# Column tiles for five matmul steps of a conv, spectral attention and FFN kernel, with a new table of times

## The chip, the cores and the metric

The kernel runs on one core of a Trainium2 chip. The metric is the device time of one execution in microseconds (us). The time before is the median of three runs; the profile is of one more execution.

## The reference

The input x is 64 images of 96 channels, 56 x 56 pixels. Two layers follow each other.

```python
# layer 0: a convolution block (MID = 192)
out = silu(bn(einsum('bchw,oc->bohw', x, expand_w)))
out = channel_shuffle(shift_groups(out), groups=4)
dw  = bn(depthwise 3x3 of out)
out = silu(bn(dw + bn(out * id_w)))
out = out * sigmoid(grouped_1x1(relu(grouped_1x1(mean(out)))))
x   = silu(bn(einsum('bchw,oc->bohw', out, proj_w)) + x)
# layer 1: on tokens t of (64, 3136, 96)
t = t + attn(layernorm(t))
t = t + ffn(layernorm(t))
```

The attention is a spectral filter: a linear map w1 to 192 hidden values with ReLU, a Fourier transform over the 3136 tokens, a complex map with a ReLU per frequency (diagonals of r and i, biases rb and ib), the inverse transform, and a linear map w2 back to 96 channels, with batch norms folded in. The FFN has 384 hidden values; the inputs and weights of its products are rounded to an 8-bit float.

## The kernel before

One image is cut into 56 kinds of steps, most of them repeated for several groups of the image. `STEPS` lists the functions, and `PLAN` gives for each call of each step a due time, relative to the image. The time of image b is moved by `b * PERIOD`. The program is written in the order of these times, and every engine carries out its own part of that order:

```python
        for _, b, k, i in sorted(
            (b * PERIOD + when, b, k, i)
            for b in range(NB)
            for k, step in enumerate(STEPS)
            for i, when in enumerate(PLAN[step.__name__])
        ):
            STEPS[k](b, i)
```

So the steps of three to four images lie among each other, and the table alone decides what stands ahead of what on an engine. Semaphores between the engines follow from the tiles that a step reads and writes.

The names of steps end in their kind: `_mm` are matmuls, `_ev` evictions of PSUM by ScalarE or VectorE. The steps that matter here, in the order of one image:

- `c_mm` and `n_mm`, by `centred` (L546): the centring products of the two layer norms. 112 tokens at a time are the stationary operand, the table `center` of 96 columns streams. Four such matmuls fill one bank of the pool `psb`; `squared` (L551, ScalarE) and `variance` (L555, VectorE) follow.
- `w1_mm` (L613): 64 columns of t are loaded for each of two halves of w1; the halves go to PSUM partitions 0 to 63 and 64 to 127.
- `f1_mm` (L640): the transform along rows, 64 columns of `buf_h` loaded of which 56 are a row, twice (real and imaginary part), 58 columns streaming.
- `f2_mm` (L666 for the first 128 hidden values, L670 for the last 64): the second transform, with `l_tab` of 112 columns streaming.
- `w2_mm` (L724 for the first 128 hidden values, L736 for the last 64, in two row halves): the map back, 112 columns of the stationary operand, 96 streaming.
- `i1_mm` (L765) and `i2_mm` (L787): the inverse transform in two steps. `i2_mm` loads 64 columns of which 48 are channels, in two tiles of 64 rows by 64 columns.

The other steps that take TensorE time are the expand products `ea_mm` (L373) and `eb_mm` (L390), the depthwise taps `dw_mm` (L436), the projection `pj_mm` (L522, L527), and the FFN: `x_mm` (L831), `h_mm` (L844), `o_mm` (L866).

PSUM is split in two. The pool `psa` has two buffers of 1024 float32 values per partition, [...] for `w1_mm`, `f1_mm`, `f2_mm`, `w2_mm`, `i1_mm` and `i2_mm`. The pool `psb` has four buffers of one bank, for all others.

## Time and profile before

| | |
|---|---|
| median of 3 runs | 7661.35 us (7661.08 to 7678.29) |
| span of the profiled execution | 7642.9 us |
| granted TensorE clock | 0.992 |
| TensorE (PE) busy | 7490.6 us |
| weight loads (PEld) busy | 5769.2 us |
| VectorE (DVE) busy | 5011.6 us |
| ScalarE (ACT) busy | 4675.8 us |
| GpSimd (POOL) busy | 1530.9 us |
| HBM read, written | 82.80 MB, 77.07 MB |

Busy time is the time in which an engine had at least one instruction at work. The matmuls overlap each other, so the busy time of a group of matmuls is not what the group costs: that is read from the distances between the starts of pieces in the timeline. A piece is a run of instructions of the same line. The chain of waits is followed back from the last instruction, and says which engine held up the end.

### The profile page before, as it was taken

The numbers are of one execution on the slowest core, as the hardware profiler recorded it, in microseconds if no ns is written. First come the engines' busy times: TensorE is split into PE (matmuls) and PEld (weight loads), VectorE is DVE, ScalarE is ACT, GpSimd is POOL, SyncE is SP. The second block draws the span as 40 slices with busy tenths as digits, with TensorE's granted clock in tenths as the row PEclk, the third lists the DMA queues.
The fourth block names the chain that finished last, engine by engine and source line by source line (L and its number), as shares of the span: only waits on it lengthen the run. The fifth ranks groups of instructions, "written<-read, shape, count | busy, mean of one in ns | idle before, by whom it ended". The sixth has DMA issues, their size and how long they took to land.

```text
span 7642.9 us, 347263 instructions
## 1 busy us (share of the span) xinstructions
PE 7490.6 (98%) x159362; PEld 5769.2 (75%) x159362; DVE 5011.6 (66%) x8793; ACT 4675.8 (61%) x9806; POOL 1530.9 (20%) x1360
## 2 busy tenths in 40 slices
PE   7999999999999999999999999999999999999997
PEld 4777777777777777777777777777777777777776
DVE  5666666666666666666666666666666666666665
ACT  3565565665665656656656566566565665665656
POOL 0111212212112122122121221221212212212112
PEclk9999999999999999999999999999999999999998
DMA  1110101101101101011011010110110101101100
GB/s 45 22 24 21 25 21 24 26 19 27 24 21 26 25 21 26 19 27 25 20 27 24 21 25 19 27 25 20 27 24 21 25 21 25 27 18 27 24 21 20
DMA packets 424192, 183.03 MB, mean 24 GB/s; under 512 B 378785, under 2 KB 422041, under 8 KB 422473
## 3 DMA queue, kind: packets, MB, share of 16 engines
q1 hardware_dynamic: 420970, 155.82, 8.9%
q8 instruction: 1251, 20.50, 1.1%
q10 hardware_dynamic: 1264, 3.48, 0.1%
q14 instruction: 211, 1.73, 0.1%
q0 software_dynamic: 496, 1.50, 0.1%
HBM read 82.80 MB, written 77.07 MB: 21 GB/s over the span
## 4 chain that ended last, share of the span: by engine, by line
PE 94%; ACT 3%; issue 1%; DVE 1%; DMA 0%; POOL 0%; POOLq 0%; SPq 0%; ACTq 0%; DVEq 0%
PE ps_d L436 13%; PE ps_f L640 10%; PE ps_w L613 8%; PE ps_i L787 6%; PE ps_eb L390 5%; PE ps_w L724 5%; PE ps_n L546 5%; PE ps_ea L373 5%; PE ps_c L546 5%; PE ps_pj L522 5%; PE ps_i L765 5%; PE ps_f L666 5%; PE ps_h L844 3%; PE ps_w L736 3%; PE ps_o L866 3%; PE ps_f L670 3%
## 5 line engine op out<-in xcount | busy, mean ns | idle before, releaser
L882 POOL TENSOR_TENSOR o<-t,o 112x448 f32<-112x448 f32 x448 | 632.7, 1418 | 4108.2 <-DVE o L876 2577.0
L555 DVE TENSOR_REDUCE v<-sq 112x4 f32<-112x384 f32 x896 | 492.7, 550 | 891.7 <-ACT sq L551 883.6
L436 PE MATMUL ps_d<-e_a,diag 32*32 32x392 f32 x36864 | 1034.3, 498 | 1.4 <-ACT d L446 0.7
L854 DVE TENSOR_SCALAR y<-y,qb 128x448 f16<-128x448 f16 x1344 | 594.3, 457 | 583.6 <-ACT y L849 575.6
L458 DVE SCALAR_TENSOR_TENSOR d_last<-e_b,taps,d_last 128x1568 f32<-128x1568 f32 x512 | 947.2, 1850 | 13.7
L436 PEld LDWEIGHTS ps_d<-e_a,diag 32*32 32x32 f32 x36864 | 661.1, 103 | 301.1 <-issue 45.1
L849 ACT CAST y<-ps_h 128x448 f16<-128x448 f32 x1344 | 715.1, 544 | 139.3 <-PE ps_h L844 137.0
L640 PE MATMUL ps_f<-f_tab,buf_h 128*64 128x58 f32 x24576 | 770.9, 223 | 0.2 <-DVE buf_h L625 0.2
L640 PEld LDWEIGHTS ps_f<-f_tab,buf_h 128*64 128x64 f32 x24576 | 737.2, 138 | 34.3 <-issue 25.8
L860 ACT CAST h<-y 128x448 fp8e5<-128x448 f16 x1344 | 739.7, 579 | 10.6 <-DVE y L854 10.2
L816 POOL TENSOR_TENSOR rs<-v,mhalf 112x4 f32<-112x4 f32 x448 | 448.9, 1007 | 1343.6 <-DVE v L556 1343.6
L613 PE MATMUL ps_w<-w1c,t 112*64 112x96 f32 x14336 | 650.8, 248 | 0.4 <-DVE buf_h L625 0.4
L613 PEld LDWEIGHTS ps_w<-w1c,t 112*64 112x64 f32 x14336 | 602.2, 137 | 18.6 <-issue 1.4
L573 POOL TENSOR_TENSOR rs<-v,mhalf 112x4 f32<-112x4 f32 x448 | 446.7, 1011 | 624.5 <-DVE v L556 624.0
L652 ACT COPY buf_g<-ps_f 128x464 f32<-128x464 f32 x768 | 395.7, 551 | 271.5 <-PE ps_f L640 263.3
L625 DVE SCALAR_TENSOR_TENSOR buf_h<-ps_w,rs_full 128x768 f32<-128x768 f32 (+1 forms) x512 | 431.4, 853 | 133.3 <-PE ps_w L613 133.2
L533 DVE TENSOR_TENSOR ps_pj<-ps_pj,x 112x392 f32<-112x392 f32 x512 | 261.4, 567 | 380.0 <-PE ps_pj L527 363.2
L551 ACT ACTIVATE sq<-ps_n 112x384 f32<-112x384 f32 x448 | 219.7, 490 | 453.5 <-PE ps_n L546 452.9
L666 PEld LDWEIGHTS ps_f<-l_tab,buf_g 128*128 128x128 f32 x3712 | 443.9, 192 | 68.7 <-ACT h L860 34.5
L546 PEld LDWEIGHTS ps_c<-center,t 112*112 112x112 f32 x3584 | 398.4, 180 | 109.1 <-ACT buf_h L776 79.8
L539 ACT ACTIVATE t<-ps_pj,pjbn_b 112x392 f32<-112x392 f32 x512 | 288.1, 618 | 308.2 <-DVE ps_pj L533 308.1
L666 PE MATMUL ps_f<-l_tab,buf_g 128*128 128x112 f32 x3712 | 462.3, 277 | 3.9 <-DVE ue L704 3.3
(174 smaller groups left out, 13514.1 us busy)
## 6 DMA issues: line engine op xcount, KB each, us to landing
x<-in_x SPq DMA_DIRECT2D x896, 84.0 KB, 2.8
out_dram<-o SPq DMA_DIRECT2D x896, 84.0 KB, 2.0
l_tab<-in_tab_l ACTq DMA_DIRECT2D x1, 1624.0 KB
r_tab<-in_tab_r ACTq DMA_DIRECT2D x1, 1568.0 KB
t<-dev_t SPq DMA_DIRECT2D x64, 7.0 KB, 1.8
t<-dev_t SPq DMA_DIRECT2D x64, 5.2 KB
ex_row_p<-in_expand_row POOLq DMA_DIRECT2D x1, 336.0 KB, 4.3
s_p<-in_bn POOLq DMA_DIRECT2D x1, 288.0 KB, 3.8
```

Of the source, the lines that this page charges most:

```text
L436: nc.tensor.matmul(pss[r][j * 32 : j * 32 + 32], lhsT=diag[pr, tap, :], rhs=e_a[pr, r0 : r0 + PJ, dx : dx + HW], start=tap == 0, stop=tap ...
L458: nc.vector.scalar_tensor_tensor(d_last, win, w, d_last, ALU.mult, ALU.add)
L546: nc.tensor.matmul(cen[:, k, 0:C], lhsT=t_of(b)[:, n0 : n0 + CP], rhs=center, start=True, stop=True)
L555: nc.vector.tensor_reduce(v, sq, AX.X, ALU.add)
L613: nc.tensor.matmul(ps[hc * 64 : hc * 64 + 64, k, 0:C], lhsT=t[:, n0 : n0 + 64], rhs=w1c[:, hc * C : hc * C + C], start=True, stop=True,)
L640: nc.tensor.matmul(ps[r * 64 : r * 64 + 64, k, 0 : 2 * NK], lhsT=buf_h[:, n0 : n0 + 64], rhs=f_tab[:, r, :], start=True, stop=True,)
L666: nc.tensor.matmul(ps[:, k, 0:CP], lhsT=g_v[:, k1, 0:128], rhs=l_tab[:, k1, :], start=True, stop=True)
L787: nc.tensor.matmul(ps[pr, bk, k, 0:HW], lhsT=buf_h[pr, n2 * 48 : n2 * 48 + 64], rhs=r_tab[pr, n2, :], start=True, stop=True,)
L849: nc.scalar.copy(y16, held.pop(("h", b, i)))
L854: nc.vector.tensor_scalar(y16, y16, qb1[:, i % 3 : i % 3 + 1], 0.0, ALU.add, ALU.max)
L860: nc.scalar.copy(held["h8", b, j][:, m, :], held.pop(("y", b, i)), saturate=False)
L882: nc.gpsimd.tensor_tensor(o32, rows, o16, ALU.add)
```

## The change

Four edits go together.

1. `c_mm`, `n_mm`, both products of `w2_mm`, and `f2_mm` for the first 128 hidden values run in two column tiles. The stationary operand is cut at column 64, and the two parts write PSUM partitions 0 to 63 and 64 up. The products are the same, the number of matmuls is doubled.
2. `f1_mm` loads the 56 columns of a row and no longer 64, and `i2_mm` loads 48 and no longer 64. The partitions in between are then not written any more, though the evictions still read them.
3. So that these partitions hold finite values from the start, the two buffers of `psa` are now fixed tiles, set to zero once, and `mix_ps` gives them out in turn.
4. `PERIOD` and `PLAN` are new: 122.718 becomes 116.056, and nearly every due time moves, so that the steps are written in another order.

The diff without the table:

```diff
+TILES = ((0, 64), (64, CP))
...
-PERIOD = 122.718
+PERIOD = 116.056
...
-    psa = ctx.enter_context(tc.tile_pool(name="psa", bufs=2, space=PSUM))
+    psa = ctx.enter_context(tc.tile_pool(name="psa", bufs=1, space=PSUM))
...
+    psa_buf = [psa.tile([128, 1024], F32, tag=f"psa_{i}", name=f"psa_{i}") for i in range(2)]
+    for ps in psa_buf:
+        nc.vector.memset(ps, 0.0)
+
+    def mix_ps(**shape):
+        psa_buf.reverse()
+        return psa_buf[0].rearrange(f"p ({' '.join(shape)}) -> p {' '.join(shape)}", **shape)
...
-            nc.tensor.matmul(cen[:, k, 0:C], lhsT=t_of(b)[:, n0 : n0 + CP], rhs=center, start=True, stop=True)
+            for c0, c1 in TILES:
+                nc.tensor.matmul(
+                    cen[c0:c1, k, 0:C], lhsT=t_of(b)[:, n0 + c0 : n0 + c1], rhs=center, start=True, stop=True
+                )
...
-        ps = psa.tile([128, 8, 128], F32, tag="psa", name="ps_w1")
+        ps = mix_ps(b=8, c=128)
...
-        ps = psa.tile([128, 16, 64], F32, tag="psa", name="ps_f1")
+        ps = mix_ps(c=16, k=64)
...
-                    ps[r * 64 : r * 64 + 64, k, 0 : 2 * NK],
-                    lhsT=buf_h[:, n0 : n0 + 64],
+                    ps[r * 64 : r * 64 + HW, k, 0 : 2 * NK],
+                    lhsT=buf_h[:, n0 : n0 + HW],
...
-                nc.tensor.matmul(ps[:, k, 0:CP], lhsT=g_v[:, k1, 0:128], rhs=l_tab[:, k1, :], start=True, stop=True)
+                for c0 in (0, 64):
+                    nc.tensor.matmul(
+                        ps[c0 : c0 + 64, k, 0:CP],
+                        lhsT=g_v[:, k1, c0 : c0 + 64],
+                        rhs=l_tab[:, k1, :],
+                        start=True,
+                        stop=True,
+                    )
...
-                nc.tensor.matmul(
-                    ps[:, u, k, 0:C],
-                    lhsT=pq_a[:, AT[k1], :],
+                for c0, c1 in TILES:
+                    nc.tensor.matmul(
+                        ps[c0:c1, u, k, 0:C],
+                        lhsT=pq_a[:, AT[k1], c0:c1],
...
-                if k < len(rows):
+                for c0, c1 in TILES if k < len(rows) else ():
                     pr = slice(u * 64, u * 64 + 64)
                     nc.tensor.matmul(
-                        ps[:, u, k, 0:C],
-                        lhsT=pq_b[pr, low[k], :],
+                        ps[c0:c1, u, k, 0:C],
+                        lhsT=pq_b[pr, low[k], c0:c1],
...
-                        ps[pr, bk, k, 0:HW],
-                        lhsT=buf_h[pr, n2 * 48 : n2 * 48 + 64],
+                        ps[oh * 64 : oh * 64 + 48, bk, k, 0:HW],
+                        lhsT=buf_h[pr, n2 * 48 : n2 * 48 + 48],
```

More of the change, by code (lines that the diff above doesn't have):

```diff
@@ L37 @@
 AT = {k: i for i, k in enumerate(ROWS)}
-PERIOD = 122.718
+PERIOD = 116.056
 PLAN = {
-    "x_in": (-147.721, -151.744, -149.471, -138.934, -151.822, -125.323, -138.247),
-    "ea_mm": (-141.029, -145.082, -126.726, -119.750, -120.807, -120.941, -120.290),
-    "ea_ev": (-138.555, -140.044, -126.163, -116.583, -120.200, -120.739, -114.561),
-    "eb_mm": (-121.730, -112.705, -108.018, -102.565, -105.002),
-    "eb_ev": (-120.973, -111.659, -106.503, -100.444, -101.911),
-    "dw_mm": (-79.917, -78.566, -78.565, -65.087, -63.669, -63.339),
-    "dw_ev": (-73.802, -73.487, -71.759, -70.033, -59.506, -57.515, -59.275, -57.457),
-    "lt": (-98.023, -96.293, -96.292, -92.859, -92.644, -88.886, -84.859, -75.675, -75.445),
-    "ls": (-61.863,),
-    "se1_mm": (-52.796,),
-    "se1_ev": (-50.943,),
-    "se2_mm": (-49.672,),
-    "se2_ev": (-48.379,),
-    "se2_th": (-46.770,),
-    "se2_pw": (-43.096,),
-    "pj_mm": (-41.772, -41.568, -32.605, -31.242),
-    "pj_add": (-40.396, -41.539, -38.890, -38.801, -31.213, -30.588, -31.045, -29.469),
-    "pj_ev": (-39.434, -38.301, -37.756, -35.301, -30.149, -29.022, -29.487, -27.900),
-    "c_mm": (-24.146, -21.968, -25.583, -16.009, -16.007, -11.503, -13.696),
-    "c_sq": (-22.682, -14.839, -23.121, -14.926, -13.660, -10.792, -11.392),
-    "c_v": (-20.883, -14.495, -18.980, -14.647, -13.137, -10.398, -11.322),
-    "c_pow": (-18.019, -14.194, -13.743, -13.702, -8.813, -8.176, -5.296),
-    "sp_v": (-10.789, -3.853),
-    "sp_mm": (-6.118, -0.681),
-    "sp_ev": (-4.506, -0.256),
-    "w1_mm": (-0.346, -0.212, 4.672, 7.510, 5.475, 12.909, 19.419, 18.928),
-    "w1_ev": (1.860, 1.106, 6.745, 17.019, 7.900, 13.580, 21.053, 22.482),
-    "f1_mm": (23.538, 26.705, 26.665, 29.311, 30.272, 32.515),
-    "f1_ev": (26.424, 25.244, 29.624, 29.156, 28.725, 26.695, 29.658, 29.859, 35.164, 35.095, 35.471, 35.913),
-    "f2_mm": (38.580, 41.391, 46.368, 52.795, 60.421, 66.169),
-    "f2_u": (40.203, 42.708, 44.419, 46.131, 57.356, 57.983, 57.453, 58.671, 64.502, 65.061, 72.435, 73.918),
-    "f2_s": (40.310, 43.807, 44.675, 46.796, 58.705, 58.706, 60.334, 60.335, 71.712, 71.894, 72.991, 75.274),
-    "f2_r": (46.995, 48.118, 58.706, 62.406, 79.686, 75.565),
-    "f2_p": (51.508, 57.047, 61.277, 69.180, 80.050, 85.487),
-    "w2_mm": (77.959, 76.224, 83.328, 86.566),
-    "w2_ev": (82.557, 79.792, 87.523, 92.017),
-    "i1_mm": (93.204, 96.670, 99.124),
-    "i1_ev": (96.030, 106.024, 102.973),
-    "i2_mm": (107.109, 107.592, 117.276, 118.471),
-    "i2_ev": (109.058, 110.782, 109.796, 112.025, 118.147, 119.865, 120.548, 122.140),
-    "n_mm": (112.633, 113.049, 118.802, 125.828, 130.991, 134.196, 139.651),
-    "n_sq": (112.809, 113.222, 120.133, 125.855, 132.488, 134.747, 139.729),
-    "n_v": (113.661, 114.505, 120.979, 128.480, 132.611, 135.903, 140.002),
-    "n_pow": (114.812, 115.024, 122.305, 128.819, 133.543, 139.096, 140.278),
-    "n_x": (117.079, 117.343, 122.642, 131.969, 137.995, 139.881, 144.238),
-    "x_mm": (118.765, 123.606, 126.764, 139.293, 142.364, 146.447, 144.732),
-    "x_ev": (122.340, 123.815, 132.084, 139.673, 148.954, 151.364, 145.152),
@@ new lines @@
+    "x_in": (-142.751, -132.334, -138.890, -139.641, -151.208, -133.652, -137.370),
+    "ea_mm": (-127.116, -124.446, -119.920, -94.498, -104.745, -112.167, -106.964),
+    "ea_ev": (-125.252, -124.279, -119.721, -94.105, -94.974, -110.456, -105.960),
+    "eb_mm": (-110.852, -109.364, -102.468, -94.672, -100.705),
+    "eb_ev": (-109.889, -108.508, -98.175, -94.671, -100.704),
+    "dw_mm": (-77.186, -75.415, -71.686, -59.708, -58.836, -58.630),
+    "dw_ev": (-67.184, -68.088, -65.354, -62.005, -53.949, -53.481, -53.376, -53.432),
@@ new lines @@
+    "lt": (-93.236, -91.843, -90.397, -86.333, -83.176, -78.618, -75.060, -71.072, -58.358),
+    "ls": (-56.957,),
+    "se1_mm": (-52.674,),
+    "se1_ev": (-52.590,),
+    "se2_mm": (-49.560,),
+    "se2_ev": (-47.764,),
+    "se2_th": (-46.882,),
+    "se2_pw": (-44.842,),
+    "pj_mm": (-44.604, -44.263, -36.259, -33.499),
+    "pj_add": (-41.623, -41.337, -40.573, -40.255, -32.468, -30.814, -32.509, -32.127),
+    "pj_ev": (-41.036, -40.637, -40.429, -36.736, -30.334, -29.230, -31.146, -29.797),
@@ new lines @@
+    "c_mm": (-24.403, -20.404, -19.123, -17.297, -18.726, -9.644, -8.872),
+    "c_sq": (-23.198, -19.663, -17.391, -16.366, -11.963, -8.651, -8.871),
+    "c_v": (-21.831, -17.939, -17.390, -11.021, -10.842, -8.366, -8.657),
+    "c_pow": (-19.058, -12.292, -10.931, -8.952, -1.526, -3.948, -1.526),
+    "sp_v": (-8.951, -1.525),
+    "sp_mm": (-6.057, 0.802),
+    "sp_ev": (-5.461, 1.113),
+    "w1_mm": (1.423, -2.619, 3.588, 18.203, 8.943, 12.171, 13.999, 16.535),
+    "w1_ev": (3.273, -0.045, 7.600, 20.920, 11.591, 14.999, 15.957, 19.212),
@@ new lines @@
+    "f1_mm": (21.608, 26.248, 24.638, 31.810, 32.559, 32.004),
+    "f1_ev": (25.169, 25.895, 30.841, 28.844, 27.556, 26.595, 32.009, 32.411, 36.910, 36.732, 36.699, 35.929),
+    "f2_mm": (37.220, 36.994, 44.528, 54.196, 60.721, 63.959),
+    "f2_u": (39.991, 41.910, 38.664, 38.665, 56.185, 56.316, 56.071, 58.643, 62.858, 62.962, 66.464, 67.055),
+    "f2_s": (42.369, 43.646, 41.684, 42.524, 58.496, 59.412, 59.011, 59.603, 66.349, 66.780, 67.365, 69.133),
+    "f2_r": (44.699, 46.227, 59.499, 60.966, 71.228, 72.985),
@@ new lines @@
+    "f2_p": (46.153, 47.154, 60.124, 60.967, 72.402, 74.345),
+    "w2_mm": (70.359, 71.061, 73.352, 79.154),
+    "w2_ev": (70.421, 73.788, 79.483, 82.773),
+    "i1_mm": (82.811, 83.639, 91.924),
+    "i1_ev": (86.931, 93.317, 99.344),
+    "i2_mm": (102.107, 101.737, 110.644, 111.766),
+    "i2_ev": (106.004, 107.037, 104.651, 104.395, 113.248, 110.645, 115.503, 113.393),
+    "n_mm": (109.042, 108.523, 116.336, 120.505, 126.604, 126.539, 137.374),
+    "n_sq": (109.105, 109.021, 116.337, 120.506, 127.174, 126.540, 137.375),
@@ L90 @@
+    "n_v": (109.642, 109.022, 116.338, 120.507, 127.975, 126.902, 138.122),
+    "n_pow": (110.809, 110.170, 116.496, 122.658, 132.126, 129.135, 139.318),
+    "n_x": (112.520, 110.693, 119.248, 123.053, 133.298, 130.929, 139.362),
+    "x_mm": (113.125, 114.113, 121.321, 126.216, 135.244, 138.382, 142.002),
+    "x_ev": (114.896, 115.709, 126.025, 126.217, 137.926, 142.365, 142.302),
     "h_mm": (
-        151.663, 153.691, 155.645, 157.017, 158.080, 157.809, 173.388, 173.148, 174.630, 194.728, 189.826, 193.482,
@@ L92 @@
-        196.505, 206.300, 207.755, 217.228, 217.688, 219.518, 219.352, 222.352, 220.276,
+        144.408, 144.539, 142.955, 151.653, 146.123, 151.741, 165.593, 167.081, 167.021, 179.037, 181.701, 184.163,
+        183.315, 191.401, 194.122, 202.572, 203.025, 214.978, 205.482, 214.132, 209.133,
     ),
     "h_ev": (
-        153.216, 154.600, 159.624, 163.665, 160.901, 163.702, 175.782, 173.779, 177.207, 198.006, 192.667, 197.471,
-        202.383, 207.982, 208.735, 217.755, 218.796, 222.132, 219.685, 226.330, 223.190,
+        146.457, 147.163, 146.728, 153.132, 153.156, 154.262, 168.465, 171.753, 169.119, 180.037, 185.733, 184.280,
@@ L97 @@
+        187.040, 192.972, 195.243, 203.531, 205.107, 216.376, 208.878, 222.205, 212.052,
     ),
     "h_b": (
-        157.149, 158.214, 159.883, 164.534, 163.184, 168.109, 177.189, 175.639, 193.423, 198.364, 197.870, 200.264,
-        208.435, 208.557, 213.046, 218.416, 218.797, 222.133, 221.871, 226.850, 225.960,
+        146.899, 148.834, 148.614, 154.505, 157.941, 159.836, 170.515, 176.287, 174.097, 185.812, 187.639, 185.918,
+        191.781, 195.030, 198.861, 204.123, 206.545, 220.428, 209.152, 226.370, 218.475,
@@ L101 @@
     ),
     "h_q": (
-        157.931, 159.867, 160.678, 169.602, 171.234, 169.760, 179.678, 181.313, 197.986, 200.300, 200.701, 203.632,
-        211.618, 213.191, 213.725, 220.633, 222.121, 228.805, 224.240, 231.019, 230.286,
-    ),
-    "o_mm": (163.728, 186.642, 207.454, 218.351, 218.341, 230.835, 234.783),
-    "o_ev": (164.829, 189.896, 208.340, 218.933, 219.309, 232.802, 234.998),
-    "o_b": (172.541, 195.548, 212.399, 222.036, 222.265, 245.929, 250.207),
-    "o_f": (177.015, 205.717, 217.170, 222.305, 225.580, 276.617, 267.685),
@@ L110 @@
-    "o_st": (192.589, 216.520, 223.872, 262.919, 254.986, 300.814, 298.874),
+        149.384, 151.139, 150.029, 159.215, 163.340, 163.159, 172.257, 183.329, 182.397, 187.024, 188.763, 189.403,
+        196.328, 198.478, 200.406, 208.755, 210.002, 221.499, 217.314, 229.791, 224.579,
+    ),
+    "o_mm": (153.028, 179.101, 192.712, 203.850, 207.474, 223.800, 230.382),
+    "o_ev": (154.015, 179.621, 193.552, 207.958, 209.955, 223.824, 232.254),
+    "o_b": (167.276, 193.254, 201.506, 209.696, 210.604, 235.187, 237.499),
@@ L111 @@
+    "o_f": (171.766, 199.519, 206.356, 219.602, 231.322, 259.139, 253.186),
+    "o_st": (197.792, 218.616, 214.282, 229.895, 257.122, 313.688, 263.438),
 }
@@ L661, in f2_mm @@
         par, _, k0, n = F2[i]
-        ps = psa.tile([128, 8, 128], F32, tag="psa", name="ps_f2")
+        ps = mix_ps(k=8, f=128)
         for k in range(n):
@@ L720, in w2_mm @@
         low, high = GROUPS[g]
-        ps = psa.tile([CP, 2, 4, 128], F32, tag="psa", name="ps_w2")
+        ps = mix_ps(u=2, k=4, o=128)[0:CP]
         for u, rows in enumerate((low, high)):
             for k, k1 in enumerate(rows):
-                nc.tensor.matmul(
-                    ps[:, u, k, 0:C],
-                    lhsT=pq_a[:, AT[k1], :],
-                    rhs=w2a,
-                    start=k == 0,
-                    stop=False,
-                    skip_group_check=True,
-                )
+                for c0, c1 in TILES:
+                    nc.tensor.matmul(
+                        ps[c0:c1, u, k, 0:C],
+                        lhsT=pq_a[:, AT[k1], c0:c1],
+                        rhs=w2a,
+                        start=k == 0,
+                        stop=False,
+                        skip_group_check=True,
+                    )
         for k in range(len(low)):
             for u, rows in enumerate((low, high)):
-                if k < len(rows):
+                for c0, c1 in TILES if k < len(rows) else ():
                     pr = slice(u * 64, u * 64 + 64)
                     nc.tensor.matmul(
-                        ps[:, u, k, 0:C],
-                        lhsT=pq_b[pr, low[k], :],
+                        ps[c0:c1, u, k, 0:C],
+                        lhsT=pq_b[pr, low[k], c0:c1],
                         rhs=w2b[pr, :],
@@ L758, in i1_mm @@
     def i1_mm(b, g):
-        ps = psa.tile([128, 16, 64], F32, tag="psa", name="ps_i1")
+        ps = mix_ps(o=16, b=64)
         for k in range(16):
@@ L779, in i2_mm @@
     def i2_mm(b, g):
-        ps = psa.tile([128, 2, 8, 64], F32, tag="psa", name="ps_i2")
+        ps = mix_ps(u=2, k=8, a=64)
         for turn in range(2):
```

## The prediction

> **What bounds the kernel now.** I read the page's part 1 first, then its chain, then the timeline of the TensorE alone in the middle of the run.

> ```profile
> PE 7490.6 (98%) x159362; PEld 5769.2 (75%) x159362; DVE 5011.6 (66%) x8793; ACT 4675.8 (61%) x9806; POOL 1530.9 (20%) x1360
> ...
> PE 94%; ACT 3%; issue 1%; DVE 1%; DMA 0%; POOL 0%; POOLq 0%; SPq 0%; ACTq 0%; DVEq 0%
> ```

> The TensorE is busy 98% of the span and holds 94% of the chain. The second engine, VectorE, has 5011.6 / 64 = 78.3 us of work per image, ScalarE 73.1 us. The depthwise pieces (L436) of image 0 and image 63 start at 56.98 and 7429.85 in the chain, 63 images apart: 117.0 us per image. In the list of waits no wait of the matmul queue apart from the start-up one of 42.9 us is above 30 us over all 64 images. So what counts is how long the TensorE takes for its own instructions. The busy column cannot give it: the durations overlap (24576 matmuls of L640 have a mean of 223 ns, or 5.5 ms if put end to end, and 770.9 us busy). I therefore take the distance from the start of one piece to the start of the next in the timeline.

> ```profile
> 3028.51 3.48 PE L787 MATMUL ps_i<-r_tab,buf_h 64*64 64x56 f32 x112
> 3031.91 0.78 PE L866 MATMUL ps_o<-h,q 128*112 128x448 fp8e5 x3
> ...
> 3034.66 1.72 PE L546 MATMUL ps_n<-center,t 112*112 112x96 f32 x16
> 3036.31 0.36 PE L587 MATMUL ps_dev<-eye,dev 112*16 112x112 f32 x2
> ...
> 3052.16 4.18 PE L613 MATMUL ps_w<-w1c,t 112*64 112x96 f32 x96
> 3056.27 1.03 PE L546 MATMUL ps_n<-center,t 112*112 112x96 f32 x8
> ...
> 3059.64 1.54 PE L613 MATMUL ps_w<-w1c,t 112*64 112x96 f32 x32
> 3061.11 1.52 PE L390 MATMUL ps_eb<-x,ex_b 112*32 112x392 f32 x16
> ...
> 3069.96 3.95 PE L640 MATMUL ps_f<-f_tab,buf_h 128*64 128x58 f32 x128
> 3073.84 0.36 PE L844 MATMUL ps_h<-xq,q 96*128 96x448 fp8e5 x1
> ...
> 3081.08 1.99 PE L666 MATMUL ps_f<-l_tab,buf_g 128*128 128x112 f32 x16
> 3082.90 0.73 PE L866 MATMUL ps_o<-h,q 128*112 128x448 fp8e5 x3
> 3083.57 1.75 PE L670 MATMUL ps_f<-l_tab,buf_g 128*64 128x112 f32 x32
> ```

> Columns: start, length, line, tile rows*columns, moving shape, records. One f32 matmul leaves two records (a c_mm of 4 matmuls shows 8), so I count records. What to see: L546 and L613 have the same 112 rows and the same 96 moving columns, and differ in the columns of the stationary operand. Sixteen records of the full tile take 3036.31 - 3034.66 = 1.65 us; thirty-two of the column tile take 3061.11 - 3059.64 = 1.47 us, although these do the same number of products.

> **Rates.** From two piece lengths each, a slope per record and a fixed part per piece:
> - L613 (two column tiles, 64 wide, 96 moving): 32 in 1.47, 96 in 4.11 us: 41.25 ns, fixed 0.15 us.
> - L546 (112 wide, 96 moving): 8 in 0.91 (3062.80 to 3063.71), 16 in 1.65: 92.5 ns, fixed 0.17.
> - L640 (two tiles, 64 wide, 58 moving): 64 in 2.01, 128 in 3.88: 29.2 ns, fixed 0.14.
> - L787 (64 wide, 56 moving): 112 in 3.40; with 0.15 fixed, 29.0 ns.
> - L666 (128 wide, 112 moving): 16 in 1.86 (the median over the run; 1.82 above), 10 in 1.10.
> - L670 (two tiles, 64 wide, 112 moving): 32 in 1.68, 28 in 1.49: 47.5 ns, fixed 0.16.
> - L724 (112 wide, 96 moving): 16 in 1.71, 10 in 1.06; L736 (64 rows, 112 wide): 16 in 0.96, 10 in 0.76.

> [...] The moving side is seen at L373: 8 records in 0.89 us, 32 in 3.12, so 92.9 ns with four column tiles at work, 372 ns for 448 columns, 0.83 ns a column: 80 ns for 96 columns, 48 for 58, 47 for 56. L613 at 2 x 41.25 = 82.5 ns per tile is then bound by its stream, its loads hidden. [...]

> **The change part by part**, per image.
> 1. c_mm and n_mm. Before: 112 records x 92.5 ns + 10.9 pieces (697 over 64 images, from the order of the built instructions) x 0.17 = 12.2 us. After: 224 records of L613's kind x 41.25 + 8.9 pieces (572) x 0.15 = 10.6 us. Saved 1.6 us, 104 us in all.
> 2. The w2a products (L724): 8 matmuls become 32 records in two tiles, 0.15 + 32 x 0.04125 = 1.47 against 1.71 us; three such groups and one of 5 matmuls (0.98 against 1.06). Saved 0.80 us, 52 us in all.
> 3. The w2b products (L736) go from two row tiles to four 64x64 tiles. No row of before has four such tiles with 96 columns. Bounds: the stream alone, 80 / 4 + 1.3 = 21.3 ns; and 27.4 ns, what L436 takes with 16 tiles (288 records in 7.89 us). I take 24.3, the middle: 0.93 against 0.96 us three times and 0.64 against 0.76 once, 0.2 us saved, 14 us in all (bounds +32 and -9).
> 4. f2_mm for fa (L666) takes L670's form: 1.68 against 1.86 us three times, no gain in the group of five. 0.54 us saved, 35 us in all.
> 5. f1_mm (L640) loads 56 columns, not 64. L640 and L787 have nearly the same rate at 58 and 56 moving columns, 58 ns per tile, above the stream (48 and 47) [...] 25.9 per record, 3.3 ns saved on each of 384 records: 1.27 us, 81 us in all. Bounds: 25.4 if only the stream is left, 29.2 if the load was not what bound it.
> 6. i2_mm (L787) loads 48. [...] i1_mm (L765, 56 moving columns, four tiles) takes 53 ns per tile, 128 records in 1.845 us less 0.15; with 49 to 53 I take 51, 25.5 per record: 3.5 ns x 224 = 0.78 us, 50 us in all. Bounds 24.6 and 29.0.
> 7. The new table cuts the work into other pieces: ea_mm goes from 254 to 443, w1_mm from 256 to 382, o_mm from 382 to 447, i1_mm from 191 to 128. At 0.147, 0.15, 0.08 and 0.14 us a piece: 28 + 19 + 5 - 9 = 43 us given back.
> 8. Two fixed PSUM buffers in turn in place of a pool of two, and two memsets of them ahead of the loop: the same depth, and the memsets stand beside start-up loads that already hold TensorE for 42.9 us. Zero. The order of instructions shows that matmuls of these steps wait for ScalarE or VectorE as before, and no longer for TensorE too. Nothing else runs on another engine than it did.

> Sum: 104 + 52 + 14 + 35 + 81 + 50 - 43 = 293 us, 4.6 us per image. All of it is on the TensorE, which has nothing to hide it: 7661 - 293 = 7368, so 7370 us, 112.4 us per image.

> **The rivals.**
> - A: full gain, no loss. The bounds of parts 3, 5 and 6 all fall well (18, 10 and 13 us more) and the finer pieces, which the new order places where one step's evictions are waited for anyway, cost half: about 7300. A table that leaves still fewer waits could give some 40 us more, 7260. For it: the idle total of before is only 152 us with start-up, so waits can't give much more. Against it: each piece of before shows the fixed part.
> - B: the narrower loads of parts 5 and 6 save nothing, because the 58 ns per tile are issue or the stream's own overhead. For it: i1_mm has 53 ns with loads of 32 columns, also above the stream. Then 131 us less is gained: 7500.
> - C: the engine is no longer fed. VectorE would be at 78.3 / 112.4 = 70% and ScalarE at 65%, and column-tiled groups fill a PSUM buffer sooner. If the evictions behind them cost 2 us per image, 7370 + 128, again 7500. Against it: the eviction of a c_mm (L551) is 0.49 us for 0.66 us of matmul, and the averages leave 30%.
> - D: slower. If the second load of a tile were not hidden in the new order (64 and 48 columns in turn, four tiles), [...] +4.3 us per image, 7940. Against it stands L613, which runs in just this manner at 41 ns.

> **How the numbers follow.** My forecast 0.55, A 0.2, B 0.1, C 0.1, D 0.05. The range from 7240 to 7470 takes in the bounds of parts 3, 5 and 6 singly and the whole of A, and leaves out B, C and D at their full size. Only D is slower. Faster by over 0.3%: 0.94, same 0.01, slower 0.05.

> **What would show it.** Right: the matmuls of c, n and w2a at 41 ns from piece to piece, 16 records of a c_mm in 0.81 us; f1's 128 records in about 3.5 us, i2's 112 in about 3.0; depthwise pieces 112.4 us apart; TensorE still at 97% or more. Wrong: f1 still at 29 ns (B), TensorE below 95% with waits for ScalarE or VectorE at the new lines (C), or c and n above 50 ns per record (D).

## The result and the profile after

The changed kernel takes 7469.69 us (7463.64 to 7473.2, four runs) against 7661.22 us, a ratio of 0.9746 with an interval of 0.9729 to 0.9763. That is 191 us less. The forecast of 7370 us was right in direction and too bold by 100 us; the time lies 0.3 us inside its range of 7240 to 7470, which is luck. All ratios below are against the kernel before, run in turn on the same chip. The median of that kernel lies between 7638.5 and 7667.2 us in the groups of runs, which is 0.4%, so I call neither of two runs of different groups faster when their ratios differ by less than that.

The page of the changed kernel, parts 1 and 4:

```profile
PE 7176.9 (96%) x177666; PEld 5259.2 (70%) x177666; DVE 4829.5 (65%) x8795; ACT 4654.4 (62%) x9806; POOL 1513.6 (20%) x1360
...
PE 85%; ACT 6%; DVE 6%; issue 3%; DMA 0%; POOL 0%; POOLq 0%; SPq 0%; ACTq 0%
```

TensorE's busy time fell by 7490.6 - 7176.9 = 313.7 us, more than was forecast. But its idle time rose from 7642.9 - 7490.6 = 152.3 to 7461.9 - 7176.9 = 285.0 us: 132.7 us are given back in waits. The chain now holds 6% of ScalarE, 6% of VectorE and 3% of "issue", where TensorE had 94% before.

The timeline of TensorE, as in the prediction (start, length, line, tile, shape, records):

```profile
3031.92 1.53 PE L745 MATMUL psa<-w2a,buf_h 128*64 128x96 f32 x32 [0.83 <-DVE ue L724]
3033.38 0.89 PE L757 MATMUL psa<-w2b,buf_h 64*64 64x96 f32 x32
3034.20 1.53 PE L745 MATMUL psa<-w2a,buf_h 128*64 128x96 f32 x32
...
3061.90 2.19 PE L557 MATMUL ps_c<-center,t 112*64 112x96 f32 x48
3064.02 0.36 PE L865 MATMUL ps_h<-xq,q 96*128 96x448 fp8e5 x1
...
3065.41 2.96 PE L808 MATMUL psa<-r_tab,buf_h 64*48 64x56 f32 x112
3068.30 0.96 PE L383 MATMUL ps_ea<-x,ex_w 112*32 112x448 f32 x8
...
3111.88 5.17 PE L653 MATMUL psa<-f_tab,buf_h 128*56 128x58 f32 x192
3116.98 0.55 PE L865 MATMUL ps_h<-xq,q 96*128 96x448 fp8e5 x2
```

Every matmul rate is as forecast or better. The 48 records of three c_mm take 2.12 us, 0.15 + 48 x 0.0413. The w2b products with four 64x64 tiles take 0.82 us for 32 records, 21 ns each, the fast bound. i2's 112 records take 2.89 us, where about 3.0 was forecast. f1's 192 take 5.10, 25.8 ns each after a fixed 0.14.

What was not forecast stands in the waits of the matmul queue (engine and line, who released it, us in total, times, longest), here of the changed kernel and then of the one before:

```profile
PE psa L786 <- issue: 108.8, 68, 2.2
PE psa L745 <- DVE ue L724: 50.8, 64, 1.7
...
PE ps_c L557 <- issue: 18.6, 20, 1.9
```

```profile
PE ps_i L765 <- issue: 29.4, 62, 2.1
...
PE ps_c L546 <- issue: 3.3, 6, 0.8
...
PE ps_w L724 <- DVE ue L704: 1.9, 3, 1.5
```

These three waits grew from 34.6 to 178.2 us, somewhat more than the whole growth of idle time, as a few others fell. The largest is a gap in the midst of a step, with no engine named:

```profile
3050.09 2.86 PE L786 MATMUL psa<-inv_tab,buf_g 112*32 112x56 f32 x216
3055.03 1.00 PE L786 MATMUL psa<-inv_tab,buf_g 112*32 112x56 f32 x40 [2.08 <-issue]
3055.96 0.93 PE L865 MATMUL ps_h<-xq,q 96*128 96x448 fp8e5 x2
3056.68 1.33 PE L887 MATMUL ps_o<-h,q 128*112 128x448 fp8e5 x3
```

Two i1_mm of 128 records each stand back to back in the new order. After 216 records, at 13 ns each, nothing starts for 2.08 us; the second i1_mm is then 216 - 128 = 88 records in, and all waits for semaphores that the trace has at this line stand at the first record of an i1_mm. The stretches around the gap (length, busy time and instructions of each engine, granted clock, share of DMA, GB/s):

```profile
3050.10:3053.00 2.90, 2.85 (x218) 2.73 (x217) 2.23 (x5) 2.20 (x5) 0.50 (x1) 1.00 0.34 69
3053.00:3055.00 2.00, 0.00 (x0) 0.00 (x0) 0.00 (x0) 0.69 (x1) 0.80 (x1) 1.00 0.54 108
3055.00:3057.00 2.00, 1.97 (x43) 1.35 (x43) 0.00 (x0) 0.45 (x2) 0.00 (x0) 0.56 0.67 162
3057.00:3059.00 2.00, 2.00 (x7) 0.99 (x5) 0.67 (x2) 1.42 (x5) 0.00 (x0) 0.58 0.51 100
3059.00:3061.00 2.00, 2.00 (x106) 1.80 (x109) 1.04 (x3) 1.52 (x4) 0.00 (x0) 1.00 0.59 153
```

The granted clock is 0.56 and 0.58 in the two stretches after the gap: the trace has it at one half for 3.41 us from 3055.26 on. The three matmuls of the o_mm at 3056.68 take 3057.80 - 3056.68 = 1.12 us, twice the 0.57 that they take after an h_mm at full clock. So a long gap can be paid for twice, but not each one is: of the 50 gaps of 1.55 us or more between 190 and 7340 us of this trace, 17 are followed by such a stretch.

### The profile page after: what moved, and what is told of

It is laid out like the page before. It is cut to its first block, busy times and chain, and to the rows that moved or that the text cites. A ratio compares the mean times of both kernels' runs of the same rounds, so it can differ in the third digit from the quotient of the medians.

```text
span 7461.9 us, 383252 instructions
## 1 busy us (share of the span) xinstructions
PE 7176.9 (96%) x177666; PEld 5259.2 (70%) x177666; DVE 4829.5 (65%) x8795; ACT 4654.4 (62%) x9806; POOL 1513.6 (20%) x1360
## 3 DMA queue, kind: packets, MB, share of 16 engines
q8 instruction: 1392, 22.81, 1.3%
q10 hardware_dynamic: 1264, 3.48, 0.1%
q14 instruction: 209, 1.71, 0.1%
## 4 chain that ended last, share of the span: by engine, by line
PE 85%; ACT 6%; DVE 6%; issue 3%; DMA 0%; POOL 0%; POOLq 0%; SPq 0%; ACTq 0%
PE psa L653 9%; PE psa L626 9%; PE ps_d L446 8%; PE ps_eb L400 5%; PE ps_ea L383 5%; PE psa L808 5%; PE ps_pj L532 5%; PE ps_c L557 5%; PE psa L745 5%; PE ps_n L557 5%; PE psa L786 5%; PE psa L680 4%; PE ps_h L865 4%; PE ps_o L887 3%; DVE s L721 3%
## 5 line engine op out<-in xcount | busy, mean ns | idle before, releaser
L875 DVE TENSOR_SCALAR y<-y,qb 128x448 f16<-128x448 f16 x1344 | 479.8, 365 | 683.9 <-ACT y L870 676.7
L653 PEld LDWEIGHTS psa<-f_tab,buf_h 128*56 128x56 f32 x24576 | 655.4, 131 | 77.8 <-DVE v L569 42.5
L626 PEld LDWEIGHTS psa<-w1c,t 112*64 112x64 f32 x14336 | 604.0, 137 | 141.4 <-DVE v L569 45.4
L653 PE MATMUL psa<-f_tab,buf_h 128*56 128x58 f32 x24576 | 688.9, 216 | 0.0
L626 PE MATMUL psa<-w1c,t 112*64 112x96 f32 x14336 | 676.2, 249 | 2.9 <-DMA t<-dev_t 1.4
L638 DVE SCALAR_TENSOR_TENSOR buf_h<-psa,rs_full 128x768 f32<-128x768 f32 (+1 forms) x512 | 435.4, 851 | 137.4 <-PE psa L626 129.5
L728 ACT ACTIVATE s<-s 128x896 f32<-128x896 f32 (+2 forms) x384 | 334.4, 887 | 288.8 <-DVE s L721 288.8
L388 ACT ACTIVATE e_a<-ps_ea 128x448 f32<-128x448 f32 x448 | 244.9, 547 | 412.5 <-PE ps_ea L383 412.5
L734 DVE SCALAR_TENSOR_TENSOR buf_h<-ue,s 128x448 f32<-128x448 f32 (+2 forms) x768 | 406.8, 580 | 109.4 <-ACT s L728 109.4
L549 ACT ACTIVATE t<-ps_pj,pjbn_b 112x392 f32<-112x392 f32 x512 | 281.4, 620 | 284.5 <-DVE ps_pj L543 284.5
L786 PE MATMUL psa<-inv_tab,buf_g 112*32 112x56 f32 x24576 | 350.5, 214 | 110.5 <-issue 108.8
```

The lines of the kernel that those rows point to most:

```text
L626: nc.tensor.matmul(ps[hc * 64 : hc * 64 + 64, k, 0:C], lhsT=t[:, n0 : n0 + 64], rhs=w1c[:, hc * C : hc * C + C], start=True, stop=True,)
L653: nc.tensor.matmul(ps[r * 64 : r * 64 + HW, k, 0 : 2 * NK], lhsT=buf_h[:, n0 : n0 + HW], rhs=f_tab[:, r, :], start=True, stop=True,)
L786: nc.tensor.matmul(ps[p0 : p0 + 32, k, 0:HW], lhsT=u_v[:, oh * 48 + o, :], rhs=inv_tab[:, r, :], start=True, stop=True,)
L875: nc.vector.tensor_scalar(y16, y16, qb1[:, i % 3 : i % 3 + 1], 0.0, ALU.add, ALU.max)
```

## The experiments

**Products or table.** Two runs part the products from the order. The first has all products of the changed kernel in the old order, the second the old products in the new order.

```diff
-PERIOD = 116.056
+PERIOD = 122.718
...
-    "x_in": (-142.751, -132.334, -138.890, -139.641, -151.208, -133.652, -137.370),
+    "x_in": (-147.721, -151.744, -149.471, -138.934, -151.822, -125.323, -138.247),
...
```

> All products as in the changed kernel (two column tiles, narrow loads, fixed PSUM buffers), but the order of before: PERIOD and PLAN are the old ones. Theory T (the new table is what ate the gain: its order leaves the TensorE waiting ahead of i1_mm and w2_mm, 160 us of waits at those two against 31 before, and cuts more pieces): the matmuls' own gain of about 390 us shows, 7270 to 7330 us. Rival S (any order shows these waits once the TensorE is faster, since evictions and instruction supply are the next limit): within 40 us of the changed kernel, 7430 to 7510. Rival N (the old order is tuned to the old durations and waits more than the new one): above 7510.

> All products as in the kernel before, with the new PERIOD and PLAN alone. Theory T: slower than before by the cost of the finer pieces (some 45 to 65 us) and by the waits at i1_mm (some 80 us), 7740 to 7800 us. Rival S: the waits come with the faster products only, so no more than the pieces' cost, 7660 to 7730.

Measured: the old order with the new products has 0.9691 (0.9673 to 0.9708), faster than the changed kernel. The new order with the old products has 1.0129 (1.0108 to 1.0151), slower than the kernel before by 0.0129 x 7661 = 99 us. So the table of times is a loss by itself: 99 us with the old products, 0.0055 x 7661 = 42 us with the new ones. The waits of the matmul queue in the second run:

```profile
PE ps_i L765 <- issue: 99.8, 60, 2.4
PE ps_w L724 <- DVE ue L704: 45.3, 62, 1.6
```

They are those of the changed kernel, with products that are as slow as before, and the time, 99 us more, is what theory T expected. Idle time there is 7762.6 - 7503.9 = 258.7 us against 152.3. The faster products did not bring these waits; the order did. But theory T expected 7270 to 7330 us of the first run, and it took 7427.79, just below the range of rival S. TensorE idles 7428.6 - 7231.4 = 197.2 us in it, 45 more than before, and the busy time fell by 259 us only. So the old order too gives back a part of what the changed lines save (373 us in the changed kernel, by the table further below; theory T's 390, and the 96 us for f1_mm in an expectation below, are too high, for f1_mm saves 82), and the next runs ask where.

**The parts.** In the old order, first the narrow loads alone, then the column tiles alone, then everything but the norms' column tiles.

```diff
+            nc.tensor.matmul(cen[:, k, 0:C], lhsT=t_of(b)[:, n0 : n0 + CP], rhs=center, start=True, stop=True)
-            for c0, c1 in TILES:
-                nc.tensor.matmul(
-                    cen[c0:c1, k, 0:C], lhsT=t_of(b)[:, n0 + c0 : n0 + c1], rhs=center, start=True, stop=True
-                )
```

This is the edit of the third run; the first also puts back w2_mm and f2_mm, the second the loads of 64 columns.

> The kernel before, order and all, with only f1_mm at 56 and i2_mm at 48 loaded columns (and the fixed PSUM buffers that these need). If the loads bound these two steps and their time is on the path: by the rates in the changed kernel's trace 96 + 68 = 164 us less, 7480 to 7520 us; by the prediction's rates 131 us less, 7530. Rival B (no gain, the time per tile is not the load): 7640 to 7665.

> Order of before, column tiles for c_mm, n_mm, w2_mm and f2_mm, but f1_mm and i2_mm load 64 columns as before. Theory D (a change of the tiling mode costs about 0.1 us, and cutting the norms' and w2's products into column tiles puts them into another mode than their neighbours h_mm, o_mm and x_mm: 79.2 changes per image against 64.5): the tiled lines give 210 us, the 14.7 added changes take back 14.7 x 0.1 x 64 = 94 us, and the first f2_mm waits some 20 to 30 us more for an eviction: 7535 to 7580 us. Rival G (no such cost; the tiled lines' gain is whole): 7440 to 7470.

> All edits and the order of before (the run of 7428 us), with c_mm and n_mm put back to whole 112-column tiles. That leaves 72.3 changes of mode per image instead of 79.2. Theory D: the norms' line loses its 85 us, the 6.9 changes fewer give back 44: 7455 to 7485 us. Rival G: 7505 to 7520.

Measured: narrow loads 0.9842 (0.9822 to 0.9861), 121 us; column tiles 0.9838 (0.9823 to 0.9854), 124 us. Together 245, and the run with both has 237: the two add up. The narrow loads give nearly what was forecast of them (131 us), so rival B, that they save nothing, is out. From start to start their two lines save 148 us, and f2_mm waits 28 us for an eviction that it hardly waited for before. (The same edit also writes fewer PSUM partitions; no run parts this from the load.)

The column tiles give 124 us, though their four lines get faster by 207; h_mm, o_mm and x_mm, which the edit doesn't touch, take 75 us more.

The norms put back to whole tiles have 0.9743 (0.9729 to 0.9758): their column tiles are worth 0.0052 x 7661 = 40 us, or 18 us by the two medians as they stand, though their own line became faster by 12.22 - 10.90 = 1.32 us per image, 84 us. By their ratios both runs fall into the ranges of theory D, the first at its edge, and both are far from rival G: column tiles make their neighbours dearer. Between the two runs with and without the norms' column tiles h_mm, o_mm and x_mm differ by 42 us.

One sees this directly. A piece of h_mm between two c_mm, in the kernel before and in the run with the old order and the new products:

```profile
3018.19 0.94 PE L546 MATMUL ps_c<-center,t 112*112 112x96 f32 x8
3018.96 0.35 PE L844 MATMUL ps_h<-xq,q 96*128 96x448 fp8e5 x1
3019.16 0.93 PE L546 MATMUL ps_c<-center,t 112*112 112x96 f32 x8
```

```profile
3052.51 0.87 PE L557 MATMUL ps_c<-center,t 112*64 112x96 f32 x16
3053.31 0.36 PE L865 MATMUL ps_h<-xq,q 96*128 96x448 fp8e5 x1
3053.60 0.88 PE L557 MATMUL ps_c<-center,t 112*64 112x96 f32 x16
```

From start to start, the same matmul of h_mm takes 0.20 us where its neighbours are whole tiles and 0.29 us where they are column tiles, and the c_mm ahead of it takes 0.77 before and 0.80 in column tiles, so that here the pair got dearer. The median over the run of an o_mm between c and n goes from 0.57 to 0.70 us, of an x_mm between eb_mm and n_mm from 0.23 to 0.33. An o_mm between two h_mm keeps 0.57. So there is a price of 0.09, 0.13 and 0.10 us in these three cases, each at a place where the tiling mode (the tile size, which I count with each side rounded up to 32, 64 or 128, so 128*128, 128*64 or 64*64) now changes and did not before. Counted in the written order, the changes go from 64.5 per image to 79.2 with the new products in the old order, and to 78.2 in the changed kernel.

**Fewer changes of mode.** The old order with the new products, and four due times moved so that h_mm and o_mm stand next to steps of their own mode (two o_ev and h_ev times move with them).

```diff
-        151.663, 153.691, ...
+        153.680, 153.691, ...
...
-        196.505, 206.300, 207.755, 217.228, 217.688, 219.518, 219.352, 222.352, 220.276,
+        196.505, 206.300, 207.755, 217.228, 217.688, 219.360, 219.352, 222.352, 222.358,
...
-    "o_mm": (163.728, 186.642, 207.454, 218.351, 218.341, 230.835, 234.783),
+    "o_mm": (163.728, 186.642, 207.454, 218.351, 218.341, 234.775, 234.783),
```

> All edits and the order of before, with four of 21 h_mm and o_mm times moved next to a step of their own mode (73.3 changes of mode per image instead of 79.2), nothing else. Theory D: 5.9 x 0.1 x 64 = 38 us less than 7428: 7375 to 7405. Rival W (the matmuls so moved come in bunches and wait for PSUM buffers and evictions, which eats it): 7420 to 7450.

Measured: 0.9719 (0.9702 to 0.9737), no faster than without the moves (0.9691, 0.9673 to 0.9708). Both theories are half right. TensorE's busy time fell from 7231.4 to 7185.6 us, 46 us, as D expects. But the bunches wait, as W says:

```profile
PE psa L786 <- issue: 49.2, 62, 2.0
...
PE ps_h L865 <- ACT y L870: 27.2, 64, 1.2
PE psa L680 <- ACT buf_g L665: 18.0, 61, 0.5
```

The waits of h_mm and f2_mm for ScalarE, 45 us, were not among the waits of the run without the moves, and i1_mm's grew by 11.

**The gap at i1_mm.** Three runs ask what it is: the second i1_mm moved away from the first, the x loads left out, and i1_mm with half as many instructions.

```diff
-    "i1_mm": (82.811, 83.639, 91.924),
+    "i1_mm": (82.811, 88.000, 91.924),
```

> The changed kernel with one due time moved: the second i1_mm goes from 83.639 to 88.000, so that two h_mm and one o_mm stand between the first and the second. Theory F (the gap of 2 us within the second i1_mm is the TensorE having no instructions: two i1_mm in a row use them up faster than the next block of instructions arrives): the gap falls to about what it was before (29 us in all, from 109), 7380 to 7410 us. Rival P (the gap is a wait for a PSUM buffer or an eviction that the trace doesn't name): the gap stays at the second i1_mm, 7455 to 7485 us.

```diff
     def x_in(b, i):
-        load_x(b, i)
+        if b < 1:
+            load_x(b, i)
```

> The changed kernel, order and all, which leaves out the loads of x for all images but the first, so that the output is not the reference's. Theory Q (the gaps at i1_mm are long because the block of instructions that the TensorE needs then is fetched while the x loads fill the DMA engines): the gaps fall from 109 us to under 50, 7390 to 7420 us. Rival R (the gaps come from the rate at which i1_mm uses instructions up, whatever the DMA engines do): 7455 to 7475.

```diff
-                for r in range(2):
-                    p0 = oh * 64 + r * 32
-                    nc.tensor.matmul(
-                        ps[p0 : p0 + 32, k, 0:HW],
-                        lhsT=u_v[:, oh * 48 + o, :],
-                        rhs=inv_tab[:, r, :],
+                p0 = oh * 64 + k % 2 * 32
+                k0 = k - k % 2
+                nc.tensor.matmul(
+                    ps[p0 : p0 + 32, k0 : k0 + 2, 0:HW],
+                    lhsT=u_v[:, oh * 48 + o, :],
+                    rhs=inv_tab,
```

> The changed kernel and its order, with the two matmuls that i1_mm makes of one stationary operand (real and imaginary part, 56 columns each) joined to one with 112 moving columns: the same columns stream through the same four tiles, with half the instructions and half the weight loads. The results land in other places of the PSUM buffer, so the output is not the reference's. Theory R (i1_mm uses instructions up faster than they come in): the gaps at i1_mm fall from 109 us to under 30 and the time to 7360 to 7400 us. Rival P (something else holds the TensorE there, a buffer or an eviction that the trace doesn't name): the gaps stay at 80 to 110 us, 7440 to 7480 us.

Measured: the one moved time gives 0.9718 (0.9697 to 0.9738). The gap at i1_mm falls from 108.8 to 67.2 us, not to 29: it breaks up, into 105 waits, and the third i1_mm has one too. The intervals of this run and of the changed kernel overlap, so whether it is faster stays open. Without the x loads the ratio is 0.9701 (0.9687 to 0.9716), 35 us less than the changed kernel and between the two theories, but the gap is still 95.3 us, where theory Q has it under 50. With those of c_mm (18.6 to 9.1) the gaps shrink by 23 of 127 us, so the loads lengthen them little.

Half the instructions in i1_mm, with the same columns streamed, give 0.9496 (0.9479 to 0.9514), 192 us less than the changed kernel. The head of its page, its longest waits, and the two i1_mm in a row:

```profile
PE 7110.7 (98%) x165378; PEld 5210.1 (72%) x165378; DVE 4833.9 (67%) x8795; ACT 4644.8 (64%) x9806; POOL 1512.4 (21%) x1360
```

```profile
PE psa L745 <- DVE ue L724: 52.1, 64, 1.7
PE ps_w1c L300 <- DVE w1s L298: 43.6, 1, 43.6
PE ps_x L852 <- DVE xt L843: 12.5, 7, 3.1
```

```profile
2972.51 3.27 PE L786 MATMUL psa<-inv_tab,buf_g 112*32 112x112 f32 x128
2975.72 0.55 PE L865 MATMUL ps_h<-xq,q 96*128 96x448 fp8e5 x2
2976.11 0.73 PE L887 MATMUL ps_o<-h,q 128*112 128x448 fp8e5 x3
```

No wait of i1_mm or c_mm for "issue" is left. The two steps take 3.21 us, or 25.1 ns for each stream of 112 columns, against 2 x 13.2 = 26.4 before, so the streaming is nearly the same. The idle time falls by 285.0 - (7262.4 - 7110.7) = 133 us, all that the new order had added. The busy time falls by 66 us: from start to start 28 of it on i1's own line, and 38 on c_mm, n_mm, h_mm and o_mm, which had run at half clock behind the gaps (the mean granted clock rises from 0.991 to 0.995). So the gap hangs on the number of instructions, not on a buffer: rival P is out. The page of the changed kernel shows how the instructions come: its instruction queue q8 moved 22.81 MB in 1392 packets, 16.4 KB each, or 64 bytes for each of the 2 x 177666 weight loads and matmuls of TensorE. That is 255.3 of these to a packet, and 256.1 with the 1163 semaphore and drain instructions that the trace has beside them.

The packets of that queue, which the trace has with their times, show the mechanism. Between 200 and 7300 us the changed kernel has 79 gaps of over 0.5 us at i1_mm and c_mm. The 62 of i1_mm come after 105 to 255 records of it in a row, but all 79 end at one and the same count of TensorE's instructions (those 1163 among them) modulo 256, so at the edge of a block of one packet's 256, and 1.17 to 1.65 us after a packet of q8 has landed. Of the 64 other waits of this length, nearly all of w2_mm, 4 end at that count. The 24 such gaps of the kernel before, and all 39 of the old order with the new products, lie at the same count. So these gaps are waits for the next block of instructions: at 13.2 ns per record i1_mm goes through a block of 128 weight loads and 128 matmuls in 128 x 13.2 ns = 1.7 us, and the next one comes later than that.

**Two attempts at a better order.** The halves of i1_mm, 32 matmuls each, are spread among the steps that follow, in the new order and in the old.

```diff
-    def i1_mm(b, g):
-        ps = mix_ps(o=16, b=64)
-        for k in range(16):
+    def i1_mm(b, n):
+        g, half = divmod(n, 2)
+        if half == 0:
+            held["i1", b, g] = mix_ps(o=16, b=64)
+        ps = held["i1", b, g]
+        for k in range(half * 8, half * 8 + 8):
...
-    "i1_mm": (82.811, 83.639, 91.924),
+    "i1_mm": (82.811, 86.520, 86.975, 88.000, 91.430, 91.924),
```

> The changed kernel with every i1_mm cut into two halves of 32 matmuls, spread between the h_mm, o_mm and c_mm that follow: same products, same output. Theory R (instruction supply): the two halves use up half as much at a time, the gaps at i1_mm and the c_mm behind it fall from 128 us to 30 to 60, and four more pieces per image cost about 0.2 us each, 51 us in all: 7410 to 7460 us. Rival (the supply is short over the whole stretch, so that the gaps only move): gaps above 90 us and the pieces' cost on top, 7480 to 7520.

> All edits and the order of before, with i1_mm cut into halves spread over the stretch from its first to past its third call: same products, same output. Theory R: the gaps of 50 us at i1_mm and c_mm there fall to about 15, the added pieces cost about 25 us: 7400 to 7430 us. Rival: no fewer gaps, 7445 to 7470.

Measured: 0.975 (0.9734 to 0.9766) in the new order, no different from the changed kernel, and 0.9734 (0.9719 to 0.9748) in the old, no faster than without the cut. The gaps at i1_mm do shrink, from 108.8 to 47.0 us and from 37.8 to 7.8. But the pieces are paid for (TensorE is busy 39 and 12 us longer), and other waits come: in the new order h_mm waits 21.9 us for an eviction by ScalarE (L549); in the old one c_mm waits 40.8 us:

```profile
PE ps_c L557 <- ACT y L872: 40.8, 59, 0.7
```

None of the runs that keep the whole computation beats the new products in the old order, 0.9691.

## Why the prediction was right or wrong

The right part is the direction and the mechanism: TensorE was the bound, and narrower stationary operands made its lines faster, together by more than was forecast. From the distances between starts, waits taken out, over 56 images in each trace (from the first depthwise piece of image 4 to that of image 60), per image and times 64:

| part | before, us per image | after | saved in all | forecast |
|---|---|---|---|---|
| 1 c_mm, n_mm | 12.22 | 10.83 | 89 | 104 |
| 2 w2a | 6.26 | 5.36 | 58 | 52 |
| 3 w2b | 3.72 | 3.08 | 41 | 14 |
| 4 f2_mm for fa | 6.66 | 6.12 | 35 | 35 |
| 5 f1_mm | 11.78 | 10.50 | 82 | 81 |
| 6 i2_mm | 6.84 | 5.78 | 68 | 50 |
| sum | | | 373 | 336 |

Part 3 came out at the fast bound, whose saving by the prediction's own lengths is 37 us and not the 32 given there. Parts 5 and 6 saved 82 and 68 us with 56 and 48 loaded columns for 64, against 81 and 50 forecast, but the lengths of a load by which part 5 is reckoned were an estimate of mine that no trace here shows. Part 1 had its time of before right (12.2); it fell short after, where c_mm stands behind the gaps of i1_mm and runs in part at half clock: with half the instructions in i1_mm, and so without gaps, the same lines take 10.54 us, as forecast (10.6). Nor do the loaded columns alone set the time of a full tile: by the prediction's own lengths L546 took 92.5 ns per record with 112 columns, L724 108 ns with the same 112, and L666 127 ns with 128. Parts 1, 2 and 4 didn't suffer, for they used the measured lengths.

The first error is in part 7, which priced only pieces that the table adds. It gave 5 us for h_mm and o_mm. The lines of h_mm, o_mm and x_mm together rose from 10.96 to 11.90 us per image, 60 us in all; 41 of them are there too in the run with half the instructions, where no gap lowers the clock. Pieces that were there before became dearer, since their neighbours are now in another mode. The fixed part that the prediction read from each piece belongs mostly to a change of mode, not to a piece: the 8 records of c_mm ahead of h_mm, both whole tiles, took 0.77 us before, only 0.03 us over 8 x 92.5 ns, where the prediction has 0.17. The column tiles make such changes where there were none. ea_mm and w1_mm rose by 40 us (47 forecast), i1_mm fell by 21 (9 forecast).

The second and larger error is that the sum has no term for waits: part 8 puts the buffers at zero, and the sentence under the sum takes all of the gain to the end. The new order added 132.7 us of idle time. This is rival C's amount, 128 us, but that is a coincidence, for C looked for evictions. One of the three waits is of that kind (w2_mm for f2's VectorE work, 49 us more); the two others (i1_mm and c_mm, 95 us more) are the gaps at the edges of instruction blocks. The prediction had the sign of it in hand, 29.4 us of "issue" at i1_mm before, and took it for small. It did not ask what happens when two of the densest steps stand back to back. Two of its own signs failed with this term: TensorE is busy 96% and not 97%, and the depthwise pieces are 114.1 us apart and not 112.4.

Taken together: 373 us saved on the six lines, 60 + 40 - 21 = 79 given back on others, 133 on waits, 21 saved on lines not named here: 182, where the spans differ by 181 and the medians by 191.

Rivals: A, the full gain, would by this sum have come to pass without the added waits and changes of mode. B is refuted by the run with narrow loads alone. D is refuted by 41 ns per record in c_mm and n_mm; the length of a load behind its 7940 us was my estimate, too.

## What to carry to other kernels

Price a change of an order apart from the change of the work it carries: here the products alone, in the order of before, are faster than both together. Column tiles made the lines that they cut faster here (c_mm and n_mm from 92.5 to 2 x 41 ns per whole tile), but put them into another tiling mode, at 0.09 to 0.13 us for a change; count the places where the mode then changes, and ask which neighbours were free of it. Where very short matmuls follow each other in hundreds (i1_mm had 13.2 ns per record), see whether the engine stands still in the midst of a step with no releaser named. If such gaps all lie at one count of its instructions modulo 256, as 79 of 79 did at i1_mm and c_mm, suspect that it lacks instructions; join matmuls of one stationary operand if their layout allows, which was worth 192 us here.
